# A MoE stage's top-k by quadrants in two halves, with the first half's gathers and experts beside the second half's selection

## The chip, the cores and the metric

The kernel runs on one core of a Trainium2 chip. The metric is device time in microseconds of one whole execution. Before the change it is 2478.52 us, the median of three runs (2477.22 to 2479.05).

## The reference, cut to what matters

The input x has 4 sequences of 1024 tokens of 256 numbers. Four stages follow one another, each added to x: windowed attention, a mixture of experts with shared experts, full attention with a layer norm behind it, and the last stage, which is the one that is changed:

```python
x = x + _L0_attn_ref(_layernorm(x), ...)
x = x + _L0_ffn_ref(_layernorm(x), ...)
x = x + _L1_attn_ref(_layernorm(x), ...)
x = x + _L1_ffn_ref(_layernorm(x), gate_w, experts)

def _L1_ffn_ref(x, gate_w, experts):          # N = 1024, E = 8, M = N // E = 128
    gate_logits = einsum('bnd,de->bne', x, gate_w)
    competitive_gates = sinkhorn(gate_logits)  # clip at 1e-6, 8 x (over tokens, over experts)
    vals, idx = top_k(swapaxes(competitive_gates, -1, -2), M)
    routed = x[b_idx, routed_indices]          # rows of the normalised x
    outputs = einsum('ebmd,edf->ebmf', routed, experts) * gate_values
    routed_back = zeros_like(x).at[b_idx, routed_indices].set(vals_bmed)
    return routed_back
```

Each of the 8 experts takes, in each sequence, its 128 tokens of highest gate, multiplies their rows by its 256 x 256 matrix, scales them by the gate, and sets them at the tokens' places. A token taken by several experts keeps the last one's row; one taken by none gets nothing.

## The kernel before, in words

x stays in SBUF as 32 tiles (`x_t`) of 128 tokens (P = 128) by 256. The last stage treats two groups of two sequences (GB = 2); a group has 16 tiles (GT) and 16 columns (GE), one for each sequence and expert. CAP = 128 is the number of slots of a column. Group 0's gates, column sums and selection are worked into the attention stage, which ends with image tile 31. What lies behind that tile is the subject here.

*Behind the attention.* `finish` (L1578) makes the attention's layer norm of a tile: two instructions on VectorE for mean and variance, then four passes of 128x256 on GpSimd, L1597 to L1602, the last of which adds into x. `gate_steps` (L1052) makes the next layer norm (xng, GpSimd, L1062), writes it to a table of rows in HBM (`xn_d`, on GpSimd's queue), turns it on TensorE, copies it on ScalarE, multiplies it by the gate weights and clips the gates (L1093, VectorE). For the last tile `lag` is 0: no pause between steps.

*Column sums.* `share_steps` (L1102): 8 iterations of five VectorE instructions around one small matmul with ones (L1113).

*Selection.* `choose_steps` (L1126): the gates are copied to `by_tile`, turned on TensorE and copied to `cur`, 16 partitions of 1024 tokens. Then 16 rounds on VectorE, each of which finds the 8 greatest of each row (L1147), their places (L1149), and replaces them by -1 (L1153, but not in the last round). The places become numbers (`top_f`, L1159), values and places are turned on TensorE, and copied to `slot_gate`, `slot_tok` and `slot_row` (L1164 to L1168): one column of 128 slots for each expert.

*Experts.* `experts_on` (L1173): column by column, an indirect DMA on GpSimd's queue gathers 128 rows (xg, L1181; six buffers, two pairs of columns ahead), TensorE turns a pair (L1219), ScalarE copies it (L1223), TensorE multiplies it by the experts (L1192), ScalarE scales it by the gate (L1202), and SyncE's queue writes it to the table `y_d` (L1206).

*Ranks.* To bring rows back, each token must know its slot. For group 1 VectorE makes for each column a 0/1 matrix of 128 slots x 1024 tokens ("hot", L1870, is_equal between `place`, 0 to 1023, and the slot's token), and TensorE sums slot numbers over it (L1872, all 16 columns into one PSUM tile of 16 partitions). ScalarE copies the sum (L1882), TensorE turns it, ScalarE copies it again (L1889). For group 0 the ranks were scattered to HBM during the attention and are only read (`read_ranks`, L1275).

*Way back.* `back` (L1232): some ten small VectorE instructions make of the ranks a row number per token (L1240 to L1257), then for each of 16 tiles an indirect DMA on GpSimd's queue gathers rows from `y_d` (yr, L1263, 8 buffers), x is added (L1269; GpSimd for group 0, VectorE for group 1), and SyncE's queue writes the output (L1270).

*Order.* The program is traced in the order of its text, and a generator is advanced step by step (`next(choose)`); a scheduler may reorder instructions of one engine, and waits between engines follow from the data. `paced(ins, other)` adds a real wait; `tc.issue_after(ins)` only orders what is traced inside it behind `ins` on the same engine. The order of the last stage is written out at its end:

```python
        run(share_steps(1, one_bank, 0))
        choose = choose_steps(1, one_bank, chosen, lambda: None)
        for _ in range(3):
            next(choose)
        experts_on(0, pool, chosen, w_all)
        for _ in range(24):
            next(choose)
        back(0, read_ranks(), "bt", nc.sync, pool)
        run(choose)
...
        experts_on(1, pool, chosen, w_all, hot_rows)
```

So group 0's experts, and then its way back, lie beside group 1's selection.

Of the kernel before, what the change touches and what calls it, by code (L numbers as in the profile page):

```python
# [8 lines left out]
F32 = mybir.dt.float32  # L9
F32R = mybir.dt.float32r  # L10
BF16 = mybir.dt.bfloat16
I32 = mybir.dt.int32
# [27 lines left out]
def two_layers(  # L40
# [1011 lines left out]
    def gate_steps(i0: int, i1: int, bank, lag: int):  # L1052
# [7 lines left out]
        for t in range(i0, i1):  # L1060
            xn = gpool.tile([P, D], F32, tag="xng", name="xng", bufs=4)
            nc.gpsimd.tensor_scalar(  # L1062
                xn, x_t[t], mv_all[:, t, 0:1], rstd_all[:, t : t + 1], ALU.subtract, ALU.mult
            )
# [108 lines left out]
    def experts_on(g: int, pool, chosen, w_all, beside=None):  # L1173

        slot_gate, _, slot_row = chosen[g]
        rows = {}

        def gather(m: int):
            for n in (2 * m, 2 * m + 1):
                xg = rows[n] = pool.tile([P, D], F32, tag="xg", name="xg", bufs=6)  # L1180
                nc.gpsimd.indirect_dma_start(  # L1181
                    out=xg[:, :],
                    out_offset=None,
                    in_=xn_d[g * GB + n // E][:, :],
                    in_offset=bass.IndirectOffsetOnAxis(ap=slot_row[:, n : n + 1], axis=0),
                )

# [21 lines left out]
        gather(0)  # L1209
        gather(1)  # L1210
        last = None
        for m in range(GE // 2 + 1):
            if m < GE // 2:
                ps = one_bank()
                for h in range(2):
                    xg = rows.pop(2 * m + h)
                    for kc in range(2):
                        c = (2 * h + kc) * P
                        nc.tensor.transpose(  # L1219
                            ps[:, c : c + P], xg[:, kc * P : (kc + 1) * P], ident  # L1220
                        )
                xgT = pool.tile([P, 4, P], F32, tag="xgT", name="xgT", bufs=3)
                nc.scalar.copy(xgT.rearrange("p k t -> p (k t)"), ps)  # L1223
                if m + 2 < GE // 2:
                    gather(m + 2)
                if beside is not None:
                    beside(m)
            if m:
                product(m - 1, last)
            last = xgT  # L1230

    def back(g: int, rank, order: str, queue, rows):  # L1232
# [3 lines left out]
        def t3(name):  # L1236
            return gpool.tile([P, GT, E], F32, tag=name, name=name, bufs=1)
# [3 lines left out]
        nc.vector.tensor_tensor(key, key, expert_no.to_broadcast([P, GT, E]), ALU.add)  # L1241
# [685 lines left out]
```

## Time and profile before

| | before |
|---|---|
| median of three runs | 2478.52 us |
| the profiled execution's own time | 2478.31 us |
| its span in the profile | 2476.3 us |
| instructions | 44321 |
| mean granted TensorE clock | 0.955 |
| PE busy | 2226.8 us (90%) |
| weight loads (PEld) busy | 1328.3 us (54%) |
| VectorE (DVE) busy | 1435.1 us (58%) |
| ScalarE (ACT) busy | 984.8 us (40%) |
| GpSimd (POOL) busy | 626.1 us (25%) |
| DMA | 205.23 MB, mean 83 GB/s |

Busy times are those of one profiled execution and overlap one another; the shares are of the span. They are means over four stages with different limits, most of the span being TensorE's attention and experts, and say little of the last stage, which begins behind 2319 us. That stage is read from the time line and from stretches of it. In it, times are counted from the span's start. The turns of the last stage, by the time line:

| what | when (us) |
|---|---|
| last tile's norms on GpSimd | 2319.72 to 2325.97 |
| group 1's column sums | 2328.5 to 2350.0 |
| group 1's selection on VectorE | 2353.01 to 2411.85 |
| its slots ready (`slot_row`) | 2413.17 |
| group 0's way back: first gather, end of the first 7 adds, end of the last add | 2367.85, 2381.2, 2398.5 |
| group 1's first gather (xg) | 2413.93 |
| its ranks copied | 2446.05 |
| its row numbers ready | 2449.08 |
| its gathers back (yr), first and last | 2449.36, 2468.72 |
| end of the span | 2476.3 |

### The profile page before, as it was taken

To read this page: it belongs to the slowest core of one execution; us is meant where nothing else is said; L and a number is where in the kernel's file an instruction comes from. 1 tells how busy PE (TensorE), PEld (TensorE's weight loads), DVE (VectorE), ACT (ScalarE), POOL (GpSimd) and SP (SyncE) were. 2 spreads that over 40 slices of the span, in tenths; PEclk is the share of its full clock that TensorE was granted. 3 is DMA by queue.
4 is the path that set the end of the run, shared out by engine and by line. 5 is a ranking of instruction groups with operands and counts; after the bars stand their busy time and mean duration, and the time that the engine had idled before them with its cause. 6 is when DMAs were issued, how large, how long until landed. Compare 5 with 4: busy or idle time off the path is not lost.

```text
span 2476.3 us, 44321 instructions
## 1 busy us (share of the span) xinstructions
PE 2226.8 (90%) x17740; PEld 1328.3 (54%) x17740; DVE 1435.1 (58%) x2371; ACT 984.8 (40%) x1354; POOL 626.1 (25%) x725
## 2 busy tenths in 40 slices
PE   6989998899999999998889999999999999999434
PEld 3555566565558888886444444444444444443222
DVE  6667665415212222223477786867777898994393
ACT  1334334111112222222115666666666565666211
POOL 1333334502430000001233222222222212124455
PEclk8999899899999999999899999999999999999667
DMA  3000000600145666663433222222221313100144
GB/s 96 20 12 14 14 16 3 208 1 30 62 136 181 212 214 207 213 212 112 100 82 84 68 54 60 54 54 60 54 61 48 66 45 70 45 19 11 56 123 136
DMA packets 202521, 205.23 MB, mean 83 GB/s; under 512 B 90584, under 2 KB 163160, under 8 KB 202316
## 3 DMA queue, kind: packets, MB, share of 16 engines
q1 hardware_dynamic: 179916, 162.32, 23.1%
q0 software_dynamic: 11584, 29.72, 4.0%
q10 hardware_dynamic: 10816, 10.36, 1.2%
q8 instruction: 140, 2.29, 0.4%
q14 instruction: 65, 0.53, 0.1%
HBM read 140.70 MB, written 56.96 MB: 80 GB/s over the span
## 4 chain that ended last, share of the span: by engine, by line
PE 66%; DVE 18%; issue 6%; ACT 5%; DMA 3%; POOL 3%; SPq 0%; POOLq 0%; ACTq 0%; DVEq 0%
PE two L1000 10%; PE two L1509 10%; PE acc L1524 8%; PE two L752 6%; DVE tops L1474 5%; PE two L1467 4%; PE acc L1027 4%; PE two L263 2%; PE two L336 2%; PE two L1389 2%; PE acc L770 2%; PE misc L770 2%; PE misc L475 1%; PE acc L431 1%; DVE top_i L1149 1%
## 5 line engine op out<-in xcount | busy, mean ns | idle before, releaser
L1474 DVE TENSOR_REDUCE tops<-two 128x2 f32<-128x1024 f32 x512 | 619.6, 1217 | 105.1 <-PE two L1467 103.1
L1517 ACT ACTIVATE pT<-two 128x1024 f32<-128x1024 f32 x512 | 523.0, 1024 | 303.0 <-PE two L1509 298.6
L1524 PE MATMUL acc<-pT,v_t 128*32 128x256 f32 x4096 | 343.0, 394 | 5.8 <-ACT pT L1517 5.6
L1509 PE MATMUL two<-q_st,k_st 64*128 64x512 f32 x1024 | 259.7, 499 | 19.4 <-ACT pT L1517 11.8
L1000 PE MATMUL two<-xbT,w_t 128*128 128x256 f32 (+1 forms) x1280 | 260.2, 359 | 1.3 <-ACT xbT L989 0.7
L752 PE MATMUL two<-xnT_f,w_t 128*128 128x512 f32 x512 | 237.1, 613 | 9.3 <-DVE tops L1474 5.2
L1000 PEld LDWEIGHTS two<-xbT,w_t 128*128 128x128 f32 x1280 | 224.3, 192 | 32.0 <-ACT xbT L989 5.3
L1467 PE MATMUL two<-k_st,q_st 64*128 64x512 f32 x1024 | 220.5, 404 | 4.5 <-DVE glu L761 1.6
L1016 DVE SCALAR_TENSOR_TENSOR glu_b<-two,b_blk,act_b 128x256 f32<-128x256 f32 (+1 forms) x160 | 72.6, 454 | 236.7 <-ACT act_b L1010 236.7
L1509 PEld LDWEIGHTS two<-q_st,k_st 64*128 64x128 f32 x1024 | 96.8, 184 | 210.0 <-issue 118.7
L1697 POOL DMA_INDIRECT yr<-ys_d,slot x64 | 62.6, 978 | 578.3 <-DMA w_raw<-in_L_attn_wk_dram 435.8
L1509 PE MATMUL two<-top_st,minus 64*128 64x512 f32 x1024 | 206.7, 396 | 0.0
L1010 ACT ACTIVATE act_b<-two,b_blk 128x256 f32<-128x256 f32 (+1 forms) x160 | 72.0, 450 | 313.3 <-PE two L1000 156.3
L1524 PEld LDWEIGHTS acc<-pT,v_t 128*32 128x32 f32 x4096 | 86.5, 108 | 166.2 <-issue 142.2
L752 PEld LDWEIGHTS two<-xnT_f,w_t 128*128 128x128 f32 x512 | 97.3, 196 | 119.4 <-issue 104.7
L1027 PE MATMUL acc<-w_t,glu_b 128*128 128x256 f32 x568 | 148.5, 390 | 8.3 <-DVE glu_b L1016 4.0
L760 ACT ACTIVATE act<-two,bT 128x512 f32<-128x512 f32 x64 | 44.0, 687 | 259.8 <-PE two L752 251.7
L1467 PEld LDWEIGHTS two<-k_st,q_st 64*128 64x128 f32 x1024 | 103.3, 185 | 73.4 <-ACT pT L1517 22.7
L416 POOL TENSOR_SCALAR_AFFINE_SELECT pT<-pT 128x1024 f32<-128x1024 f32 x64 | 70.4, 1100 | 269.5 <-ACT pT L413 262.2
L413 ACT ACTIVATE pT<-two 128x768 f32<-128x768 f32 (+1 forms) x128 | 93.5, 783 | 95.5 <-PE two L336 95.4
L1027 PEld LDWEIGHTS acc<-w_t,glu_b 128*128 128x128 f32 x568 | 102.1, 189 | 35.0 <-DVE glu_b L1016 23.6
L1569 POOL TENSOR_TENSOR y<-y,rows_b 128x256 f32<-128x256 f32 x32 | 23.5, 735 | 366.9 <-DVE y L1566 366.9
(314 smaller groups left out, 3141.0 us busy)
## 6 DMA issues: line engine op xcount, KB each, us to landing
w_t<-in_L_ffn_rw_dram SPq DMA_DIRECT2D x120, 512.0 KB
halves<-split SPq DMA_DIRECT2D x64, 256.0 KB
q_st<-halves SPq DMA_DIRECT2D x128, 128.0 KB
k_st<-halves SPq DMA_DIRECT2D x256, 64.0 KB
xb<-xs_d SPq DMA_DIRECT2D x31, 256.0 KB
ys_d<-yb ACTq DMA_DIRECT2D x31, 256.0 KB
xs_d<-zeros SPq DMA_DIRECT2D x5, 1536.0 KB
b_t<-in_L_ffn_rb_dram SPq DMA_DIRECT2D x40, 128.0 KB
```

Source lines behind the costliest of these rows:

```text
L413: nc.scalar.activation(pt[:, 2 * ab : 2 * ab + 2, :, :n], scs[ab], AF.Exp)
L752: mm(ps[:, n * 512 : (n + 1) * 512], lhsT=w_t[:, kc, f * P : (f + 1) * P], rhs=xnT[:, kc, cols], start=(kc == 0), stop=(kc == 1),)
L770: mm(ps[:, jj * D : (jj + 1) * D], lhsT=glu[:, f, j * P : (j + 1) * P], rhs=w3_t[:, f, :], start=(f == 0), stop=(f == NF - 1),)
L1000: mm(ps[:, m * 512 + ff * cols : m * 512 + (ff + 1) * cols], lhsT=w_t[:, kc, f * P : (f + 1) * P], rhs=xbT[:, kc, :cols], start=(kc == 0), ...
L1010: nc.scalar.activation(act[:, :cols], ps[:, ff * cols : (ff + 1) * cols], AF.Silu, bias=b_blk[0][:, f, n : n + 1],)
L1016: nc.vector.scalar_tensor_tensor(glu[:, f, :cols], ps[:, 512 + ff * cols : 512 + (ff + 1) * cols], b_blk[1][:, f, n : n + 1], act[:, :cols ...
L1027: mm(ps[:, a * D : (a + 1) * D], lhsT=glu[:, f, a * P : (a + 1) * P], rhs=w3_t[:, f, :], start=(f == 0), stop=(f == NF - 1),)
L1467: mm(sc[:, hh], lhsT=q_st[rows, j * P : (j + 1) * P], rhs=k_st[rows, kk * 512 : (kk + 1) * 512], start=True, stop=True,)
L1474: newest["vector"] = nc.vector.tensor_reduce(tops[:, :, j, kk], sc, AX.X, ALU.max).ins
L1509: mm(sc[:, hh * 512 : (hh + 1) * 512], lhsT=minus[rows] if top else k_st[rows, k * P : (k + 1) * P], rhs=(top_ring[p % 2] if top else q_st ...
L1517: newest["scalar"] = nc.scalar.activation(pt, sc, AF.Exp).ins
L1524: newest["tensor"] = mm(oT_ps[32 * r : 32 * r + 32, hh * D : (hh + 1) * D], lhsT=vals[n // HU][:, n % HU, k, :], rhs=pts[r // 2][:, hh * 5 ...
```

## The change

Only the last stage and the last tile ahead of it are touched.

- The last tile's four attention-norm passes and its xng go from GpSimd to VectorE. The making of `place` waits for that xng.
- Group 0's 16 gathers are all issued ahead of group 1's column sums, into 16 buffers, and its experts take them from there.
- `choose_halves` takes the place of `choose_steps` for group 1. The gates are doubled, so that `cur` starts with 32 partitions (each column twice). Round k reads and fills quadrant k // 4 of the partitions and slot k % 4 of the free dimension; the replacement writes into the next slot or quadrant, so that all 16 states of the array stay. Places are then searched not once per round but for a whole half (8 rounds, 64 partitions) in four instructions. So there are 16 MAX8, 15 replacements and 8 searches, and slots 0 to 63 are known after half of the rounds. Eight small matmuls with columns of the identity deliver a half's values and places, so that one column of 128 partitions holds 64 slots of two neighbouring experts: 8 columns per half.
- Each half then has 8 gathers, 4 pairs of columns through `half_experts`, products into 64 partitions each, and 16 writes of 64 rows to `y_d`: 32 writes for group 1 instead of 16. The first half's are placed beside the second half's selection.
- The ranks of the first half are made of signs: ScalarE computes Sign(place - token + 0.5), TensorE sums it with half the slot number as weight, ScalarE copies the sums beside a first column with their value left of token 0, and VectorE takes the difference of neighbouring columns (`rank_half`), which is the slot number at its token and 0 elsewhere. The second half's 0/1 matrices are made on VectorE as before, and their sum is added to `rank_half` sequence by sequence. Row numbers are made sequence by sequence (`sources`).
- Group 0's way back is split on GpSimd's queue into 7, 7 and 2 tiles, with 8 gathers of group 1 behind the first and behind the second part; it has 16 buffers. Its outputs are written by SyncE in two lots (`put_taken`), the first behind the first half's writes to `y_d` and the rest behind the second's. Group 1's 16 additions stand behind all row numbers on VectorE.

The diff, cut to its core:

```diff
+    def choose_halves(g: int, bank, chosen, after, pool, parts: int = 2):
...
+        by_tile = pool.tile([P, TB, 2, GE], F32, tag="by_tile", name="by_tile", bufs=1)
+        for n in range(2):
...
+        cur = pool.tile([P, 4, S], F32, tag="cur", name="cur", bufs=1)
+        for hf in range(2):
...
+            nc.vector.tensor_copy(cur[:32, 0, hf * 512 : (hf + 1) * 512], ps[:32, :])
...
+        def of_round(k: int):
+            return slice(32 * (k // 4), 32 * (k // 4) + 32), k % 4
...
+        for k in range(rounds):
+            q, a = of_round(k)
+            behind(nc.vector.max, out=top_v[q, a, :], in_=cur[q, a, :])
+            yield 0
...
+                behind(
+                    nc.vector.match_replace,
+                    out=cur[q1, a1, :], in_to_replace=top_v[q, a, :], in_values=cur[q, a, :],
+                    imm_value=-1.0,
...
+            if (k + 1) % (rounds // parts):
+                continue
+            part = (k + 1) * parts // rounds - 1
+            rows = slice(part * P // parts, (part + 1) * P // parts)
+            for a in range(4):
+                behind(
+                    nc.vector.max_index,
+                    out=top_i[rows, a, :], in_max=top_v[rows, a, :], in_values=cur[rows, a, :],
...
+            behind(nc.vector.tensor_copy, top_f[rows], top_i[rows])
...
+                    for h in range(parts):
+                        row = 64 * h + 32 * (j % 2) if parts == 2 else 32 * j
...
+                            mm(
+                                ps[row : row + 32, k0 * n : (k0 + 1) * n],
+                                lhsT=top[q].rearrange("p a i -> p (a i)"),
+                                rhs=ident[q, 32 * j + h : 32 * j + GE : parts],
...
+            nc.vector.tensor_copy(slot_tok, ps[:, n : 2 * n])
+            nc.vector.tensor_copy(slot_row, slot_tok)
+            nc.scalar.copy(slot_gate, ps[:, :n])
+            chosen[g, part] = slot_gate, slot_tok, slot_row
+            after()
...
+    def take_rows(slots, columns, pool):
+
+        xgs = []
+        for b, n in columns:
+            xg = pool.tile([P, D], F32, tag="xg", name="xg", bufs=16)
+            ga = nc.gpsimd.indirect_dma_start(
+                out=xg[:, :],
+                out_offset=None,
+                in_=xn_d[b][:, :],
+                in_offset=bass.IndirectOffsetOnAxis(ap=slots[2][:, n : n + 1], axis=0),
+            )
+            xgs.append(xg)
+        newest["rows"] = ga.ins
+        return xgs
...
+    def half_experts(g: int, part: int, m: int, xgs, pool, w_all):
+
...
+        with ExitStack() as order:
+            if part:
+                order.enter_context(tc.issue_after(newest["ranks"]))
+            xgT = turned(xgs, pool)
...
+                    half = slice(64 * h, 64 * h + 64)
+                    mm(
+                        ps[half, c * D : (c + 1) * D],
+                        lhsT=xgT[:, 2 * c + kc, half],
+                        rhs=w_all[:, (2 * (m + c) + h) % E, kc, :],
+                        start=(kc == 0),
+                        stop=(kc == 1),
...
+            for h in range(2):
+                row = ((2 * (m + c) + h) % E) * CAP + 64 * part
+                newest["outputs"] = nc.sync.dma_start(
+                    out=y_d[g * GB + b][row : row + 64, :], in_=yg[64 * h : 64 * h + 64, :]
+                ).ins
...
+        src_row = gpool.tile([P, GT], I32, tag="src_row", name="src_row", bufs=2)[:, :n]
+        newest["numbers"] = nc.vector.tensor_copy(src_row, src_f).ins
+        return src_row
...
+    def back(b: int, t: int, src_row, n: int, adder, rows):
+
+        i = b * TB + t
+        yr = rows.tile([P, D], F32, tag=f"yr{b // GB}", name="yr", bufs=16)
...
+        adder.tensor_tensor(yr, yr, x_t[i], ALU.add)
+        taken.append((i, yr))
...
+    def put_taken():
+
+        with tc.issue_after(newest["outputs"]):
+            for i, yr in taken:
+                nc.sync.dma_start(out=out_rows[i * P : (i + 1) * P, :], in_=yr)
+        taken.clear()
...
+                v = nc.gpsimd if lag else nc.vector
+                v.tensor_scalar(
...
+                v.tensor_tensor(ys[j], ys[j], gamma_b, ALU.mult)
+                v.tensor_tensor(ys[j], ys[j], beta_b, ALU.add)
+                v.tensor_tensor(x, x, ys[j], ALU.add)
...
+        paced(
+            nc.gpsimd.iota(place_i, pattern=[[1, S]], base=0, channel_multiplier=0).ins, last_xn[0]
+        )
...
+        slot_col = wpool.tile([P, 2, E // 2, E], BF16, name="slot_col")
         nc.gpsimd.memset(slot_col, 0.0)
...
+            half = slice(64 * h, 64 * h + 64)
+            for part in range(2):
+                nc.gpsimd.tensor_scalar(
+                    slot_col.rearrange("p n m e -> p n (m e)")[half, part, h :: E + 2],
+                    slot_i[half, part, :], 0.5 + 0.5 * part, None, ALU.mult,
+                )
...
+        sums_to = wpool.tile([RB, 1 + S], F32, name="sums_to")
+        nc.gpsimd.memset(sums_to, 0.0)
+        nc.gpsimd.memset(sums_to[:, 0:1], -0.5 * (64 * 65 // 2))
...
+        xgs0 = take_rows(chosen[0], columns, pool)
         run(share_steps(1, one_bank, 0))
...
+        choose = choose_halves(1, one_bank, chosen, lambda: ready.append(0), wpool)
+        for _ in range(4):
             next(choose)
-        experts_on(0, pool, chosen, w_all)
-        for _ in range(24):
...
+        for _ in range(8):
             next(choose)
-        back(0, read_ranks(), "bt", nc.sync, pool)
+        src_row = sources(read_ranks(), GT)
...
+        def some_back(n: int):
+            with tc.issue_after(newest["rows"]):
+                for _ in range(n):
+                    b, t = next(rest)
+                    back(b, t, src_row, b * TB + t, nc.gpsimd, pool)
...
+
+            tok = chosen[1, part][1][:, m : m + 1]
+            hot = pool.tile([P, S], BF16, tag="hot", name="hot", bufs=3)
+            if part:
+                newest["hot"] = nc.vector.tensor_scalar(hot, place, tok, None, ALU.is_equal).ins
+            else:
+                nc.scalar.activation(hot, place, AF.Sign, bias=half_less[:, m : m + 1])
+            b, mb = divmod(m, E // 2)
...
+                newest["ranks"] = mm(
+                    rank_ps[32 * b : 32 * b + E, hf * 512 : (hf + 1) * 512],
+                    lhsT=slot_col[:, part, mb, :],
+                    rhs=hot[:, hf * 512 : (hf + 1) * 512],
...
+        some_back(7)
+        while not ready:
+            next(choose)
+        half_less = wpool.tile([P, E], F32, name="half_less")
+        nc.vector.tensor_scalar(half_less, chosen[1, 0][1], -1.0, 0.5, ALU.mult, ALU.add)
+        xgs = take_rows(chosen[1, 0], columns, pool)
+        for m in range(0, E, 2):
+            half_experts(1, 0, m, xgs[m : m + 2], pool, w_all)
+            for c in range(2):
+                ranks_of(0, m + c)
+            next(choose)
+        for b in range(GB):
+            nc.scalar.copy(sums_to[32 * b : 32 * b + E, 1:], rank_ps[32 * b : 32 * b + E, :])
+        put_taken()
+        some_back(7)
         run(choose)
...
+        xgs = take_rows(chosen[1, 1], columns, pool)
+        some_back(2)
+        src_rows = []
+        for b in range(GB):
+            for m in range(b * E // 2, (b + 1) * E // 2, 2):
+                for c in range(2):
+                    ranks_of(1, m + c)
+                half_experts(1, 1, m, xgs[m : m + 2], pool, w_all)
+            mine = slice(32 * b, 32 * b + E)
+            if b == 0:
+
+                rank_half = wpool.tile([RB, S], F32, name="rank_half")
+                with tc.issue_after(newest["hot"]):
+                    nc.vector.tensor_tensor(
+                        rank_half, sums_to[:, 1:], sums_to[:, :S], ALU.subtract
                     )
-
...
+            rankT = pool.tile([P, S], F32, tag="rankT", name="rankT")
+            nc.vector.tensor_tensor(rankT[mine], rank_ps[mine, :], rank_half[mine], ALU.add)
...
+            nc.scalar.copy(rank.rearrange("p n e -> p (n e)"), ps[:, : TB * E])
+            src_rows.append(sources(rank, TB))
+
+        with tc.issue_after(newest["numbers"]):
+            for b in range(GB):
+                for t in range(TB):
+                    back(GB + b, t, src_rows[b], t, nc.vector, pool)
+        put_taken()
```

## The prediction

> **What bounds the kernel now.** I read the page first, then the chain of waits from 2300 us on, then a table of stretches cut at that chain's turns. The diff leaves everything up to the last image tile's layer norm (2319 us) as it stood, instruction for instruction on every engine, so only the end of the run counts. Columns of the table: stretch, length, busy us and instructions of PE, weight loads, VectorE (DVE), ScalarE (ACT) and GpSimd (POOL), TensorE clock, DMA share, GB/s.
>
> ```profile
> 2299.00:2328.50 29.50, 14.29 (x70) 8.55 (x70) 5.92 (x28) 11.28 (x17) 19.70 (x25) 0.65 0.20 58
> 2328.50:2350.00 21.50, 4.68 (x16) 4.02 (x16) 14.07 (x48) 0.00 (x0) 5.18 (x6) 0.50 0.26 82
> 2350.00:2353.00 3.00, 2.61 (x12) 1.67 (x12) 1.58 (x3) 0.00 (x0) 0.00 (x0) 0.50 0.00 0
> 2353.00:2413.20 60.20, 19.27 (x96) 16.14 (x95) 58.43 (x82) 10.72 (x24) 36.00 (x42) 0.67 0.42 127
> 2413.20:2446.30 33.10, 29.54 (x136) 18.35 (x135) 11.89 (x16) 11.98 (x26) 16.25 (x16) 0.94 0.40 120
> 2446.30:2449.40 3.10, 0.00 (x0) 0.00 (x0) 2.34 (x11) 0.02 (x1) 0.04 (x1) 0.74 0.26 85
> 2449.40:2476.30 26.90, 0.00 (x0) 0.00 (x0) 6.81 (x16) 0.00 (x0) 15.87 (x16) 0.50 0.54 156
> ```
>
> Five stretches follow one another with one busy engine each: the selection of group 1 (DVE, 60.2 us), its gathers, experts and ranks (PE, 33.1), the row numbers (3.1), and the way back (16 gathers on POOL, 26.9). Group 1's TensorE work waits for the whole selection. Then the rows that price an operation (count, busy us, mean ns):
>
> ```profile
> L1263 POOL DMA_INDIRECT yr<-y_d,src_row x32 | 31.1, 972 | 25.3 <-DVE src_row L1257 14.6 <-issue 8.8 <-DMA out_dram<-yr 1.5
> L1147 DVE MAX8 top_v<-cur 16x8 f32<-16x1024 f32 x16 | 19.5, 1217 | 0.5
> L1149 DVE FIND_INDEX8 top_i<-top_v,cur 16x8 uint32<-16x1024 f32 x16 | 19.3, 1205 | 0.0
> L1153 DVE MATCH_REPLACE8 cur<-top_v,cur 16x1024 f32<-16x1024 f32 x15 | 18.0, 1197 | 0.0
> L1149 DVE MATCH_VALUE_LOAD top_i<-top_v,cur 16x8 f32 x16 | 1.3, 79 | 0.5
> L1153 DVE MATCH_VALUE_LOAD cur<-top_v,cur 16x8 f32 x15 | 0.9, 59 | 0.0
> ```
>
> A round is 1.217 + (1.205 + 0.079) + (1.197 + 0.059) = 3.757 us; 16 rounds less one replacement make 58.8 us, which is 2353.0 to 2411.85 in the time line. A gather holds POOL for 0.95 us and the next starts 1.25 us after it.
>
> **The change, part by part.**
>
> *Last tile's norms from POOL to DVE.* Before, the four steps on y and x ran on POOL from 2319.72 to 2323.35, then xng waited behind place_i and slot_col and ended at 2325.97. A DVE pass over 128x256 takes 0.40 to 0.43 us. In DVE's new queue the third step stands behind a gates copy that PE delivers only at 2321.8, so x is ready at 2322.95, a gain of 0.4; xng then ends at 2324.6. Gain 1.4 us, all on the path. The moved memsets and constants, and 16 gathers instead of 6, run on POOL under the 21.5 us of column sums: 20 us of gathers and 4 of constants from 2323 end near 2348.5, and their first reader comes at 2351. A longer POOL eats that slack first.
>
> *Doubled by_tile.* One copy more (0.23) and some waits ahead of it and of its transposes, say 0.2: the selection starts at 2353.0 - 1.4 + 0.4 = 2352.0.
>
> *Quadrants.* MAX8 and replacements stay (16 and 15); index searches fall from 16 to 8, since one serves two quadrants. 16 x 1.217 + 15 x 1.256 + 8 x 1.284 = 48.6 us, 10.2 less. First half: 9.7 + 10.0 + 5.1 = 24.9, second 23.7. No row shows these operations on 32 or 64 partitions; the nearest, by length, is a reduction of 128x1024 at 1.217 us, the very time of MAX8 on 16x1024, so I take no cost for partitions (below nothing is excluded: the elements per partition are the same; above, see the rivals):
>
> ```profile
> L1474 DVE TENSOR_REDUCE tops<-two 128x2 f32<-128x1024 f32 x512 | 619.6, 1217 | 105.1 <-PE two L1467 103.1
> ```
>
> First slot_row: 2352.0 + 24.9 + 0.2 (top_f) + 1.24 (the next MAX8 stands ahead) + 0.2 + 1.26 (a replacement too) + 0.2 = 2380.0. Second: 2352.0 + 48.6 + 0.7 (first half's small copies) + 1.3 (as 2411.85 to 2413.17 before) = 2402.6, against 2413.17: 10.6 us gained.
>
> *First half's work beside the second selection.* ACT gets 8 Signs (128x1024; a same-sized Exp takes 1.02), 4 casts of 0.59, 8 scalings of 0.42 and two copies of 1.0: 16 us inside 22.6. PE has less. Cost nothing while the second slots come after 2400; were DVE faster, ACT's two copies would be late next. The first half's sum on TensorE leaves the end; in its place DVE gets one subtraction over 40x1024 and two additions over 8x1024, about 1.1 us each by the ACT copy of 16x1024 (1.0), between its hots, while gathers are awaited.
>
> *POOL's queue.* In order: 7 back gathers and adds of group 0, 8 gathers, 7 and 7 again, 8 gathers, 2 and 2, then the 16 of the end. Before, the first seven and their adds took 2367.85 to 2381.2; all comes 0.9 earlier, so the first half's gathers go 2380.4 to 2390.4. Seven of each cost 7 x 1.25 + 7 x 0.75 = 14.0, to 2404.4: the second slots, ready at 2402.6, wait 1.8 us for POOL. While DVE ran hots, the gathers came late:
>
> ```profile
> 2415.22 1.02 POOL L1181 DMA_INDIRECT xg<-xn_d,slot_row  x1 [0.30 <-PE two L1872]
> 2416.54 1.23 POOL L1181 DMA_INDIRECT xg<-xn_d,slot_row  x1 [0.30 <-issue]
> 2418.07 1.44 POOL L1181 DMA_INDIRECT xg<-xn_d,slot_row  x1 [0.30 <-PE two L1872]
> 2419.81 0.94 POOL L1181 DMA_INDIRECT xg<-xn_d,slot_row  x1 [0.30 <-DMA xg<-xn_d,slot_row]
> ```
>
> From the one at 2413.93 that is 5.9 us for four, 0.9 over 4 x 1.25. [...] I take the row. The eighth gather then starts at 2404.5 + 8.75 + 0.9 = 2414.2, two back gathers follow, the last lands 3.1 later, and its add ends at 2420.6.
>
> *TensorE in the second half.* 8 gathers, not 16; each carries two experts' 64 rows, and the products use half the columns of the array. Here the value sums of the attention show such halves:
>
> ```profile
> 2094.97 1.97 PE L1429 MATMUL misc<-wv_t,xnT_a 128*64 128x128 f32 x32
> ```
>
> 32 in 1.9 us is 59 ns each, against 107 for a full 128-column pass (half of the 213 that 256 columns take in L1192): neighbours overlap. So a pair of columns costs as before, 1.9 us. Pair 0 waits for gather 2 (lands 2409.4), is cast and multiplied by 2412.3; gather 4 (2411.9), rank transposes (0.7) and hots (1.4), pair 2 to 2416.4, scaling 0.9, four writes of 64 rows at 0.52 each (x loads: 32 in 16.74 us), landing 2.4: y of sequence 2 is complete at 2420.7. [...] Before, eight products took 2.77 us cold against 1.89. All cold would be 2424.5, all warm 2420.7; half of the work lies under landings, so I take 2422 for the first back gather.
>
> *The end.* Sequence 3's pairs end near 2422, its 8 writes land at 2427, and the ninth gather wants them at 2432. Its numbers (2.7 us after ACT's rank copy) come at 2425.7, when the first gathered rows have just landed at 2425. So the back stretch stays 26.9 us, plus 0.5 for nine outputs of group 0 held until then (0 to 1.5; they pass at 0.52 us each, ahead on SP, and SP has 25 writes, 13 us, in 25). 2422 + 26.9 + 0.5 = 2449.4.
>
> **Sum.** Span 2476.3 to 2449.4, 26.9 us less: 1.4 - 0.4 + 9.6 (selection net of small copies) to the second slots, then 36.2 us from slots to first back gather become 19.4 (16.8), less 0.5. The profiled run took 2478.31, 2.0 over its span and 0.2 under the median: **2451.4 us**.
>
> **Rivals.**
> [...]
> 2. *TensorE or ScalarE is late* (15): cold all through, or halves that don't overlap (1.9 becomes 3.7 for pairs 0 and 2), or a table switch around Sign (the order of instructions has none): 3 to 6 us, 2455 to 2458.
> 3. *The slower side* (3): DVE's searches cost more with 32 and 64 partitions, or by writing into the next quadrant. Place: the 48.6 us of selection, which nothing covers. Doubled, the run takes 2500; it decides from 55% more, 1.9 us per operation. Against: the 128-partition row above.
> 4. *Better* (10): POOL and PE both on time and warm, back gathers at 1.25 instead of 1.29 as the buffers no longer run out: 2446.
> 5. *The halves don't overlap* (2): a queue holds the first half back, leaving selection and norms: some 11 us, 2467.
>
> **Numbers.** My case takes the other 53. A measurement can tell about 0.2%, 5 us. Range 2445 to 2461: down to rival 4, up through rival 2 to rival 1's value. Faster 0.95, same 0.02, slower 0.03.
>
> **What would show it.** In the new trace: 31 selection steps of 1.2 us and 8 searches of 1.28; second slot_row near 2402.6; products of 64x256 at about 115 ns; a POOL without idle time from 2380 to 2417; the first of the last 16 gathers at 2422; 27 us after it. Wrong if searches take longer, gathers stand over 1.5 us apart, or that first gather comes after 2430.

## The result and the profile after

The changed kernel takes 2463.89 us (median of 5 runs, 2460.76 to 2469.79) against 2478.52 us (5 runs, 2472.63 to 2480.81): a ratio of 0.9951, 95% interval 0.9932 to 0.9969. The forecast was 2451.4, with a range up to 2461: the direction was right, the gain 14.6 us instead of 27. The profiled execution took 2465.89 us with a span of 2464.1.

The stages ahead of the change take up to 19 us more or less from one trace to another, so traces are laid over one another at one point that the change does not touch: the start of the last tile's output product (between 2297.3 and 2316.7 us in the traces below). It stands in the time lines of before and after (start, length, engine, line):

```profile
2313.00 2.07 PE L1563 MATMUL misc<-wo_t,cT 128*128 128x256 f32 x4 [0.46 <-ACT cT L1559]
```

```profile
2309.30 2.07 PE L1700 MATMUL misc<-wo_t,cT 128*128 128x256 f32 x4 [0.46 <-ACT cT L1696]
```

From there to the end it was 163.3 us before and is 154.8 after. That is 8.5 us less; 3.7 more of the difference between the two profiled spans come from the stages ahead. The table of stretches of after, cut at its own turns (columns as in the prediction):

```profile
2323.35:2345.49 22.14, 4.67 (x16) 4.01 (x16) 14.71 (x48) 0.00 (x0) 17.03 (x18) 0.50 0.51 154
2345.49:2348.57 3.08, 2.62 (x12) 1.76 (x12) 1.72 (x4) 0.00 (x0) 0.00 (x0) 0.50 0.05 19
2348.57:2377.96 29.39, 18.42 (x110) 15.64 (x108) 28.66 (x39) 10.91 (x25) 11.55 (x14) 0.85 0.33 103
2377.96:2399.96 22.00, 12.32 (x58) 5.56 (x59) 21.46 (x29) 7.56 (x10) 17.23 (x20) 0.66 0.35 97
2399.96:2410.45 10.49, 8.25 (x54) 3.90 (x53) 0.34 (x3) 7.11 (x12) 1.95 (x3) 0.63 0.26 60
2410.45:2434.86 24.41, 20.40 (x106) 9.45 (x107) 11.87 (x22) 6.38 (x14) 13.39 (x12) 0.72 0.46 125
2434.86:2464.10 29.24, 0.53 (x8) 0.43 (x7) 8.57 (x27) 0.94 (x3) 15.49 (x16) 0.56 0.68 201
```

The first half's selection, the second's, and the last gathers have the lengths that were forecast, within 2 us. The row that should not be there is the fifth: 10.5 us between the end of the selection and the second half's slots, with VectorE at 0.34 busy us and TensorE at 8.25. The selection itself, by groups (count, busy us, mean ns):

```profile
L1217 DVE MAX8 top_v<-cur 32x8 f32<-32x1024 f32 x16 | 19.5, 1219 | 0.5
L1217 DVE MATCH_REPLACE8 cur<-top_v,cur 32x1024 f32<-32x1024 f32 x15 | 18.0, 1203 | 0.1
L1217 DVE FIND_INDEX8 top_i<-top_v,cur 64x8 uint32<-64x1024 f32 x8 | 9.6, 1219 | 0.0
```

On 32 and 64 partitions they cost what they cost on 16 before (1217, 1197 and 1205 ns). Where the 10.5 us come from is read in three time lines of after: VectorE's, ScalarE's and TensorE's.

```profile
2399.74 0.22 DVE L1217 CAST top_f<-top_i 64x32 f32<-64x32 uint32 x1
2410.07 0.17 DVE L1262 COPY slot_tok<-misc 128x8 f32<-128x8 f32 x1 [10.11 <-PE misc L1252]
```

```profile
2390.63 2.19 ACT L2038 ACTIVATE hot<-place,half_less 128x1024 bf16<-128x1024 f32 x2
2399.82 0.84 ACT L1350 ACTIVATE yg<-two,slot_gate 128x256 f32<-128x256 f32 x2 [7.01 <-remote]
```

```profile
2390.99 1.95 PE L1340 MATMUL two<-w_all,xgT 128*64 128x256 f32 x16
...
2394.94 0.66 PE L1290 MATMUL acc<-ident,xg 128*128 128x128 f32 x4
2401.75 1.01 PE L2041 MATMUL two<-hot,slot_col 128*8 128x512 bf16 x2 [6.15 <-ACT hot L2038]
2402.69 6.12 PE L1340 MATMUL two<-w_all,xgT 128*64 128x256 f32 x32
2408.74 1.03 PE L2041 MATMUL two<-hot,slot_col 128*8 128x512 bf16 x4
2409.69 0.24 PE L1252 MATMUL misc<-ident,top_v 32*32 32x8 f32 x8
```

TensorE multiplied the first half's second pair by 2392.94 (modelled end) and went on to turn rows. ScalarE, free at 2392.82, scaled that product only at 2399.82; "remote" means that the profile names no releaser. Its instruction waited for TensorE's semaphore alone (S[110] in the trace, which TensorE's instructions raise), and in the trace's semaphore events TensorE's update came at 2399.80, with three later ones within 0.2 us. Ends on TensorE are modelled, so the trace does not tell whether the product itself was late or only its report; it is called a late report here. Behind the stalled scaling stand signs and copies in ScalarE's queue, behind those TensorE's rank sums and products, and behind these, in its queue, the small matmuls that deliver the second half's slots (L1252). VectorE had finished at 2399.96 and waited for them. This is "the wait" of what follows.

### The profile page after: what moved, and what is told of

The parts are those of the page before. It is cut to its first block, busy times and chain, and to the rows that moved or that the text cites. A ratio compares the mean times of both kernels' runs of the same rounds, so it can differ in the third digit from the quotient of the medians.

```text
span 2464.1 us, 44521 instructions
## 1 busy us (share of the span) xinstructions
PE 2233.8 (91%) x17842; PEld 1325.7 (54%) x17842; DVE 1430.0 (58%) x2370; ACT 995.1 (40%) x1366; POOL 625.8 (25%) x726
## 4 chain that ended last, share of the span: by engine, by line
PE 66%; DVE 16%; issue 6%; ACT 5%; POOL 3%; DMA 2%; SPq 1%; another core or an unknown queue 0%; ACTq 0%; POOLq 0%; DVEq 0%
PE two L1000 10%; PE two L1646 10%; PE acc L1661 8%; PE two L752 6%; DVE tops L1611 5%; PE two L1604 4%; PE acc L1027 4%; PE two L263 2%; PE two L336 2%; PE two L1526 2%; PE acc L770 2%; PE misc L770 2%; PE misc L475 1%; PE acc L431 1%; ACT pT L1654 1%
## 5 line engine op out<-in xcount | busy, mean ns | idle before, releaser
L1611 DVE TENSOR_REDUCE tops<-two 128x2 f32<-128x1024 f32 x512 | 619.4, 1217 | 103.5 <-PE two L1604 101.2
L1646 PE MATMUL two<-q_st,k_st 64*128 64x512 f32 x1024 | 260.1, 500 | 19.4 <-ACT pT L1654 11.8
L1010 ACT ACTIVATE act_b<-two,b_blk 128x256 f32<-128x256 f32 (+1 forms) x160 | 72.1, 451 | 313.2 <-PE two L1000 161.8
L1604 PEld LDWEIGHTS two<-k_st,q_st 64*128 64x128 f32 x1024 | 103.2, 185 | 73.6 <-ACT pT L1654 22.7
```

The costliest lines, as they stand in the source:

```text
L1010: nc.scalar.activation(act[:, :cols], ps[:, ff * cols : (ff + 1) * cols], AF.Silu, bias=b_blk[0][:, f, n : n + 1],)
L1604: mm(sc[:, hh], lhsT=q_st[rows, j * P : (j + 1) * P], rhs=k_st[rows, kk * 512 : (kk + 1) * 512], start=True, stop=True,)
L1611: newest["vector"] = nc.vector.tensor_reduce(tops[:, :, j, kk], sc, AX.X, ALU.max).ins
L1646: mm(sc[:, hh * 512 : (hh + 1) * 512], lhsT=minus[rows] if top else k_st[rows, k * P : (k + 1) * P], rhs=(top_ring[p % 2] if top else q_st ...
```

## The experiments

All are measured from the start of the last tile's output product, in us. "Gap" is from the end of the last top_f to the end of the second slot_row, "slots to back" from there to the first of the last 16 gathers. Runs e1 to e4, e5 to e8, e9 to e11, e12 to e14 and e15 to e18 were made together, each group on one chip.

| run | chip | gap | second slots | slots to back | back to end | end |
|---|---|---|---|---|---|---|
| before | | 1.1 | 100.2 | 36.2 | 26.9 | 163.3 |
| forecast | | | 89.6 | 19.4 | 27.4 | 136.4 |
| after | | 10.5 | 101.1 | 24.4 | 29.3 | 154.8 |
| e1_repeat | 8 | 10.2 | 100.8 | 24.4 | 27.6 | 152.8 |
| e2_outputs14 | 8 | 10.2 | 100.0 | 24.3 | 25.9 | 150.2 |
| e3_no_signs | 8 | 6.5 | 97.1 | 22.2 | 26.3 | 145.7 |
| e4_norms_gpsimd | 8 | 9.7 | 103.9 | 22.7 | 26.7 | 153.3 |
| e5_back_late | 3 | 1.2 | 91.2 | 31.1 | 26.4 | 148.6 |
| e6_yg8 | 3 | 2.0 | 91.8 | 20.1 | 25.8 | 137.8 |
| e7_writes_late | 3 | 2.0 | 91.8 | 21.0 | 25.4 | 138.2 |
| e8_halves_apart | 3 | 1.3 | 91.4 | 22.5 | 25.8 | 139.7 |
| e9_repeat2 | 7 | 1.3 | 91.9 | 22.1 | 26.4 | 140.5 |
| e10_yg8_again | 7 | 2.0 | 92.0 | 20.2 | 26.4 | 138.6 |
| e11_yg8_outputs14 | 7 | 1.3 | 91.1 | 22.4 | 25.8 | 139.2 |
| e12_repeat3 | 15 | 10.1 | 100.2 | 20.0 | 27.1 | 147.3 |
| e13_fill | 15 | 10.1 | 99.8 | 20.3 | 26.8 | 146.9 |
| e14_hots_behind | 15 | 10.3 | 101.0 | 30.1 | 26.3 | 157.3 |
| e15_repeat4 | 3 | 1.3 | 91.9 | 22.6 | 26.2 | 140.7 |

**The changed kernel again (no edit), and again.** First run:

> The changed kernel once more, nothing edited. In its first trace ScalarE stood idle for 7.0 us in the middle of the first half's work (2392.8 to 2399.8, in front of the scaling of the second pair) until TensorE reported a product whose modelled end lay at 2392.9, and the second half's slots came 10 us after their selection had ended. My theory, that the first half's chain of ScalarE and TensorE is too long for its cover whatever happens: the same gap of some 9 to 10 us between the end of the selection (the last top_f) and slot_tok here, and about 2464 us. The rival, a stall that belongs to that one execution: the gap is 1 to 4 us here, the profiled time 6 to 8 us lower, near 2457.

The 10 us came back, 2456.10 us against 2473.66 (ratio 0.9937, 0.9919 to 0.9954); the wait was 6.9 us. So it was no accident of one execution. On later occasions:

> The changed kernel a third time, beside a kernel that did not show the 7 us. Four different edits all came out without that wait, so it may belong to a chip or to an hour and not to the kernel. If the wait is the kernel's own (ScalarE's scaling of the second pair behind TensorE's report): again 9 to 10 us between the last top_f and slot_row, and 146 us or more from the last tile's output product to the last output. If it belongs to the conditions of the earlier runs: slots 1 to 2 us after top_f, and about 134 to 136 us.

Here the wait was gone: 2455.83 us against 2470.69 (ratio 0.9920, 0.9896 to 0.9944). VectorE's, ScalarE's and TensorE's time lines of that run:

```profile
2404.54 0.23 DVE L1217 CAST top_f<-top_i 64x32 f32<-64x32 uint32 x1
2405.35 0.17 DVE L1262 COPY slot_tok<-misc 128x8 f32<-128x8 f32 x1 [0.59 <-PE misc L1252]
```

```profile
2395.19 2.18 ACT L2038 ACTIVATE hot<-place,half_less 128x1024 bf16<-128x1024 f32 x2
2397.35 0.84 ACT L1350 ACTIVATE yg<-two,slot_gate 128x256 f32<-128x256 f32 x2
```

```profile
2400.42 3.67 PE L1340 MATMUL two<-w_all,xgT 128*64 128x256 f32 x32
```

The same two instructions of ScalarE follow one another at once, and the slots' first copy starts 0.6 us after the selection. TensorE's next two pairs took 3.67 us at the full granted clock; in after, behind the wait, they took 6.12, since the granted clock was at half until 2407.7. Then:

> The changed kernel a fourth time. So far its trace showed the 7 us wait of ScalarE on two occasions and not on a third, with nothing edited, and every variant run beside it went the same way as the others of its occasion. If the wait belongs to the chip: this run and the variants beside it all show it or all lack it; with it slots come 9 to 10 us after top_f and 149 us lie between the tile's output product and the last output, without it 1 to 2 us and 136 us.

The wait was there again, in all three kernels of that group (2457.73 us against 2475.47, ratio 0.9939, 0.9920 to 0.9959). The last repeat was the control of a set meant to find the cause:

> The changed kernel unedited, as the control of this set. On chips 8 and 15 every trace had the wait of some 7 us, on chips 3 and 7 none. With it: slots 9 to 10 us after top_f. Without it: 1 to 2 us, and the three variants beside it then tell nothing of its cause.

It was on chip 3 again and lacked the wait. So the set, in which the late writes (end 138.7) and the late way back (149.4) were tried once more and a late second selection (161.8) for the first time, tells nothing of it. Its expectations:

> All 16 writes of the first half are issued after its last scaling (8 row buffers of their own). If the control shows the wait: it stays at 7 us if SyncE's writes have nothing to do with it, and slots come 1 to 3 us after top_f if they cause it.

> The middle seven of group 0's gathers and adds stand behind the second half's gathers, so GpSimd is idle at that time. If the control shows the wait: it stays at 7 us if GpSimd's gathers and adds have nothing to do with it, and slots come 1 to 3 us after top_f if they cause it.

> The second half's selection starts only when the first half's sums are copied, so VectorE is idle beside the first half's products (their order on TensorE changes a little with it). If the control shows the wait: it stays, as a gap of 7 us between a product's end and its scaling, if VectorE's selection has nothing to do with it, and it is gone if it causes it. The run is longer either way by the lost overlap: the second selection then starts 12 to 25 us later.

The last of them shows what the overlap is worth: with the second selection begun only behind the first half's sums, the slots come at 115.9 instead of 91.9.

**Fourteen outputs written early.**

```diff
-        put_taken()
-        some_back(7)
+        some_back(7)
+        put_taken()
         run(choose)
```

> 14 of group 0's 16 outputs, instead of 7, are written behind the first half's writes; 2 instead of 9 are held until the end. In the changed kernel's trace SyncE's queue issued 25 outputs from 2438.7 to 2461.6, many 1.4 us apart, and the last went out 4 us after its row was ready. If the held outputs are what lengthens the last stretch (29.2 us from the first of the last 16 gathers to the end, against 26.9 before): 26 to 27 us there, 2 to 2.5 us less, about 2462. If the end is bound by the gathers and the DMA engines alone: 29 us still, no change.

From the first of the last gathers to the end it took 25.9 us beside 27.6 on the same chip: 1.7 less. In the timed runs (2458.12 beside 2456.10) that is lost in the spread of 9 us.

**No signs.** The edit drops ranks_of(0, ...) and the two copies to sums_to, and sets the first column of sums_to to 0. It leaves out the rows of group 1's tokens in the first half's slots.

> Leaves out the first half's ranks: no signs on ScalarE, no sums of them on TensorE, no copies of the sums; the subtraction and the additions stay, on zeros, so tokens of the first 64 slots of group 1 get no row. If the second slots are late because the first half's rank work shares in-order queues with its products: slots within 2 us of the selection's end, and 7 to 9 us less than the changed kernel in the same call, about 2456. If the lateness comes from the products, the gathers or a stall of TensorE apart from the signs: slots still 6 us or more late, and at most 2 us less.

The gap fell only from 10.2 to 6.5: ScalarE's scaling of the second pair again waited, 8.35 us, with no sign ahead of it. The rank work lengthens the delay by 3.7, but does not bring the wait about. Timed, 2456.06 us beside 2456.10.

**Norms on GpSimd again** (nc.gpsimd in both places for every tile).

> The last tile's norms are back on GpSimd, all else as changed. The prediction gave this move 1.4 us, the traces of before and after show 15.5 and 14.05 us from the tile's output product to the first column sum. Theory: 1 to 3 us more than the changed kernel (its xng now stands behind a gather too), about 2466. Rival: GpSimd's queue of gathers and constants is moved ahead and nothing is lost: no change.

The column sums start 3.8 us later (17.8 instead of 14.1): xng stands behind a gather and constants. At the end of its trace 0.5 us are left of it, since this trace took 1.7 us less from slots to back (22.7 against 24.4 in e1) and 0.9 less in its last stretch; timed, 2466.43 us beside 2456.10, which is more than the trace accounts for. At equal granted clock (the estimate at the end of the next section) the timed runs are some 5 us apart.

**Four tries at the wait.** In back_late the middle some_back(7) goes behind the second take_rows; yg8 gives the halves' scaled rows 8 buffers of their own:

```diff
-            yg = pool.tile([P, D], F32, tag="yg", name="yg", bufs=4)
+            yg = pool.tile([P, D], F32, tag="yh", name="yg", bufs=8)
```

writes_late has these buffers too and issues the first half's writes behind its last scaling; halves_apart swaps the loops over h and kc in a product.

> The middle seven of group 0's gathers and adds on GpSimd go behind the second half's eight gathers, so that GpSimd is free while the first half's second pair is multiplied. In all five traces of the changed kernel and its variants ScalarE's scaling of the second pair waits some 7 us past the modelled end of its product. If those gathers and adds, with their transfers, are what holds it: the wait falls under 2 us and the slots come within 3 us of the selection's end. If not: 7 us again. The whole run is not shorter either way, since 7 gathers and adds (14 us) now stand ahead of the last ones.

> The halves' scaled rows get 8 buffers of their own instead of sharing 4 with group 0, so the scaling of the first half waits for no write to the table; nothing else moves. If that wait is the cause of the 7 us (the trace would then have named the wrong releaser): it is gone, slots 7 us earlier, 2449 to 2457. If ScalarE really waits for TensorE: 7 us again, no change.

> As with 8 buffers, and the first half's 16 writes of 64 rows are all issued after its last scaling, so that no write runs beside the products. The 7 us begin, in four of five traces, while the first four writes are issued. If the writes hold TensorE or ScalarE: no wait of 7 us here, slots within 3 us of the selection's end. If not: 7 us again.

> In a product the two matmuls of one half of the columns follow one another before those of the other half, so that neighbours in the queue use the same half in pairs. If the report of a product comes late because both halves of the array are in flight together: the wait of 7 us goes or changes, and a product takes longer (up to 3.7 us instead of 1.95 at the full clock). If the order of halves has nothing to do with it: 7 us again, with products within 0.3 us of the changed kernel's.

All four lacked the wait. Taken by themselves they would have "proved" four causes; the unedited kernel lacks it on that chip too, so none is shown. e8 settles its own question besides: with the two matmuls of one half next to each other, 16 matmuls took 3.74 us at half the clock and 2.00 at the full one, nearly as in the other order (3.68 and 1.95).

**Eight buffers, timed.**

> The version with 8 row buffers of its own once more, timed. If buffers removed the wait: 134 us again from the output product to the last output and 10 to 14 us less than the changed kernel beside it. If the conditions did: the same as the changed kernel beside it, within the noise of 3 us.

> 8 row buffers and 14 outputs of group 0 written behind the first half's writes. With the first half on time SyncE's queue had 23 to 24 us from the first of the last 16 gathers to the last output in the version with 8 buffers, as before the change, so the outputs should now add nothing: the same as 8 buffers alone within 1 us if the queue had already caught up, 2 us less if the nine held outputs still cost something.

2449.94 us and 2447.53 us, beside 2455.83 for the changed kernel and 2470.69 before (ratios to before 0.9898, 0.9874 to 0.9922, and 0.9899, 0.9878 to 0.9920). In the traces they end at 138.6 and 139.2 instead of 140.5. The two intervals overlap, and both overlap that of the changed kernel beside them (0.9896 to 0.9944), so a gain over it is not shown. Nor do 8 buffers remove the wait: e13 and e14 have them, and the wait.

**TensorE kept warm; VectorE kept quiet.** Warm means that TensorE's full clock is granted, cold that half of it is. Both edits stand on top of e11's kernel. The core of the first, which also puts the second half's rank sums behind the filling:

```diff
+        fill = one_bank()
+        with tc.issue_after(newest["slots"]):
+            for _ in range(8):
+                newest["fill"] = mm(fill, lhsT=ident, rhs=place[:, :512], start=True, stop=True).ins
         xgs = take_rows(chosen[1, 1], columns, pool)
```

> With 8 row buffers and 14 outputs written early; besides, 8 matmuls of 128x512 whose result nobody reads stand on TensorE behind the second half's slots, where it waits some 4 us for gathers. Theory, that the second half is late by its cold clock: the four products take 1.9 us per pair, the first of the last 16 gathers comes 2 to 4 us earlier than in the same kernel without them (112.0 us after the tile's output product), 3 us less in all. Rival, that the second half waits for GpSimd's gathers and the rank sums: same place within 1 us.

Slots to back took 20.3 us, against 22.4 without the filling on chip 7, but the unedited kernel beside it took 20.0: the run by itself decides nothing. All traces together tell more, though by comparison only, since no edit sets the clock. The second half's first pair of columns, in TensorE's time line of after and of e13:

```profile
2419.15 3.68 PE L1340 MATMUL two<-w_all,xgT 128*64 128x256 f32 x16
...
2424.33 2.72 PE L2041 MATMUL two<-hot,slot_col 128*8 128x512 bf16 x6
2426.99 2.50 PE L1340 MATMUL two<-w_all,xgT 128*64 128x256 f32 x16
```

```profile
2418.46 1.95 PE L1340 MATMUL two<-w_all,xgT 128*64 128x256 f32 x16
...
2422.47 1.95 PE L1340 MATMUL two<-w_all,xgT 128*64 128x256 f32 x16
```

Where the full clock was granted from the first pair on (e6, e10, e12, e13; 1.00 over the pair in e12 and e13), slots to back is 20.0 to 20.3; where the first pair ran at half the clock and the second at the full one (e3, e4, e8, e9, e11, e15; 0.52 and 1.00 in e9), 22.1 to 22.7; in after, e1 and e2, where the second pair began cold too (0.50 and 0.77 in after), 24.3 to 24.4. In e7 the first pair turned warm midway: 21.0. The same program falls into any of the three: unedited, it is in all of them (e12; e9 and e15; after and e1). The second edit:

```diff
                 newest["hot"] = nc.vector.tensor_scalar(hot, place, tok, None, ALU.is_equal).ins
+                if m == 0:
+                    paced(newest["hot"], newest["rows"])
```

> With 8 row buffers and 14 outputs written early; VectorE's first 0/1 matrix of the second half waits for the eighth gather, so GpSimd gathers while VectorE is idle. If VectorE's work is what stretches the eight gathers (11.2 to 11.6 us from the first to the last start, 8.75 at the spacing of 1.25): 8.75 here. The products wait for the ranks in TensorE's queue, so the end comes 6 to 10 us later: a probe, not a remedy. If the stretch has another cause: 11 us again.

GpSimd's eight gathers took 8.8 us from the first start to the last, as expected if VectorE's work stretches them; in after it is 11.2. GpSimd's time line of after, and part of VectorE's:

```profile
2412.46 1.02 POOL L1274 DMA_INDIRECT xg<-xn_d,slot_row  x1 [0.30 <-PE two L2041]
2413.79 2.15 POOL L1274 DMA_INDIRECT xg<-xn_d,slot_row  x1 [0.30 <-issue]
2416.24 0.95 POOL L1274 DMA_INDIRECT xg<-xn_d,slot_row  x1 [0.30 <-issue]
2417.49 0.94 POOL L1274 DMA_INDIRECT xg<-xn_d,slot_row  x1 [0.30 <-issue]
2418.74 2.09 POOL L1274 DMA_INDIRECT xg<-xn_d,slot_row  x1 [0.30 <-issue]
```

```profile
2413.24 1.21 DVE L2078 TENSOR_TENSOR rank_half<-sums_to 40x1024 f32<-40x1024 f32 x1
2414.38 0.73 DVE L2036 TENSOR_SCALAR hot<-place,slot_tok 128x1024 bf16<-128x1024 f32 x1
```

The two long ones lie beside the subtraction with a 0/1 matrix behind it, and beside two 0/1 matrices (2418.61 to 2420.00); others beside such matrices took 0.96 and 1.02. Both long ones end 0.83 us after the last VectorE instruction beside them (2415.94 after 2415.11, 2420.83 after 2420.00), and an undisturbed gather takes 0.95: they were held nearly from their start until VectorE was through. Over all traces, 27 of the last stage's 29 gathers of more than 2 us end 0.81 to 0.84 us after a VectorE instruction.

## Why the prediction was wrong, point by point

- **Last tile's norms: right.** From the output product to the first column sum 14.1 us instead of 15.5: 1.4, as forecast. e4 adds that GpSimd, with its new queue of gathers and constants, would have made it 17.8.
- **Column sums with 16 gathers on GpSimd: right.** They ended at 2344.4, before the selection, and held nothing up. One two-input instruction of VectorE took 0.91 us instead of 0.29 while GpSimd cast `place`, and the column sums 22.1 us instead of 21.5.
- **Selection: right, 2 us long.** It was put at 48.6 us and 0.9 of small copies; from its first MAX8 to the end of the last top_f it took 51.4. The first top_f took 1.04 where 0.2 was assumed, and between a replacement and the next MAX8, and between that and the load behind it, 0.03 us pass (in after a MAX8 from 2348.57 ends at 2349.79, the load starts at 2349.82).
- **"Cost nothing while the second slots come after 2400": the step that failed.** The sum of ScalarE's work (16 us inside 22.6) was right, and on chips 3 and 7 its cover held: gap 1.3 (e9, e15). In the first trace the gap was 10.5, 9.2 more than that: 6.9 of the late report, and about 2.4 of the next two pairs, which then found TensorE at half the clock (6.12 us instead of 3.67). The term left out is not work but a report: TensorE's semaphore for a finished product came 7 us late, in the first trace and all traces of chips 8 and 15, and in none of 3 and 7. The step had named what would be late next (ScalarE's two copies), not that the slots' matmuls stand behind the whole first half in TensorE's queue, where the late report's 6.9 us were paid in full.
- **TensorE in the second half: half right.** The column halves overlap as forecast: 16 matmuls in 1.95 us at the full clock (1.9 was taken), 3.68 at half. The clock was taken as half cold at 1.3 us (2422 instead of 2420.7), an estimate from eight products before, 2.77 and 1.89 us; what makes the clock fall is not shown by any run. By the three levels of slots to back (20.0 to 20.3, 22.1 to 22.7, 24.3 to 24.4) it costs 0, 2 or 4, and 4 in the first trace.
- **GpSimd's gathers beside VectorE: undersized.** Taken at 0.9 by the row of before; 2.4 here (11.2 less 8.8), 1.7 to 3.6 in the other traces of the changed kernel and its variants, e14 apart. Two of the eight in after were held until the VectorE instructions beside them were through, and lasted 2.15 and 2.09 us; the other six took 0.94 to 1.02. The wait of the second slots for GpSimd's queue was 1.4 us in e9, where 1.8 was forecast.
- **The end: undersized.** 0.5 for nine held outputs; the stretch was 29.3 instead of 27.4, and 1.7 of it went with seven outputs written early (e2 against e1). In the unedited kernel without the wait it was 26.4 and 26.2.
- **The rivals.** The second, TensorE or ScalarE late by a cold clock, named the right engines, but had 3 to 6 us for what became 13 (9.2 and 4). The fifth, a queue that holds the first half back, is the nearest in kind, but the halves did overlap: without the overlap (e18) the slots come 24.0 us later. The first, GpSimd as the bound (17 in 100; 24 gathers 1.74 us apart, 10 us more, 2461, the top of the range), came at most for the eight late gathers, 1.60 us apart on average in after; the last 16 stood 1.27 us apart there, and no run shows 1.74 over 24 gathers. (Its sum is off by its own figures: 1.74 less 1.25 is 0.49 for each of 24, 11.8 and not 10.) The slower side did not come.

Without the late report the trace of e9 ends at 140.5: 4.1 over the forecast of 136.4 and 22.8 under before's 163.3. With it, after gains 8.5. The timed runs lie closer together than that (2455.83 on chip 7, 2456.10 and 2457.73 on chips 8 and 15): beside before they gain 14.9, 17.6 and 17.7 us, so the medians do not show the wait, and on chip 7, where the trace lacks it, the timed gain is still well short of the 27 forecast: how much of the miss in the medians the wait makes is not shown. Much of their spread goes with the granted clock of the whole run. Over the 41 timed runs of before made beside the experiments, a straight line gives 1.45 us less for each 0.001 of clock and leaves 2.2 us of spread. Measured from that line, the changed kernel's runs are shorter by 9.2 us on average in the first measurement, 12.0 on chip 8, 13.0 on chip 15 and 17.6 on chip 7. This is an estimate, and chips may differ in other things, but it goes the way of the wait. Whether each timed run had it is not known, since only one execution of each kernel is traced.

What stays open is why the report is late, and why on some chips. Signs are excluded as its cause (e3, a wait of 8.35 us without them), and so are the shared buffers (e13, e14, gaps of 10.1 and 10.3 with 8 buffers). The writes, GpSimd's gathers and VectorE's searches could only be taken away on a chip that does not show it. In each of the eight affected traces semaphore events of ScalarE's instructions just ahead of the wait are missing, though SyncE acted in time; the other eleven traces have theirs. In after they are those of five instructions, which end between 2386.60 and 2392.82, and SyncE issued the first write of the scaled rows at 2390.18, 0.02 us after the first scaling's end. So the wait may belong to the recording of events and not to the kernel; this is the author's guess, and no run here tests it.

## What to carry to other kernels

Work that is hidden beside a search is only hidden if nothing that the search's result needs stands behind it in a queue: price the deliverer's place, not only the sum of the work (in after, behind a report 6.9 us late, the gap was 10.5 us instead of 1.3). Lay traces over one another at a point that the change does not touch before comparing them: here that took out up to 19 us that have nothing to do with the change. And repeat the unedited kernel beside its variants: four edits each "removed" a wait that the kernel itself did not have on that chip.

## What the runs showed of the hardware

- MAX8 and its replacement over 1024 elements take 1.20 to 1.22 us on 16 (before) and on 32 partitions (after), the index search 1.21 to 1.22 on 16 (before) and on 64 (after).
- TensorE's report of a finished fp32 product came 6.7 to 7.2 us after its modelled end at the same place in all eight traces of the first measurement and chips 8 and 15, and in none of eleven on chips 3 and 7; the same eight lack semaphore events of ScalarE there (five in after).
- Indirect gathers on GpSimd start 1.25 us apart beside an idle VectorE (e14) and beside MAX8 searches (after, 2378.70 to 2387.49), and 2.0 to 3.3 us instead of 0.95 are taken by single ones beside 0/1 matrices and two-input operations (2.15 and 2.09 in after); 27 of 29 such end 0.81 to 0.84 us after a VectorE instruction.
